# Where the own keys of a second attention get their norm: in the projection stage, or as a factor on the scores

## The chip, the core and the metric

The kernel runs on one core of one Trainium2 chip. The time is the device time of one execution in microseconds. The kernel before took 2516.35 us (median of three runs, 2516.21 to 2521.84 us).

## The reference, cut to what matters

One decoder layer on 8 sequences of 100 tokens with 1024 features: a retention block, a second attention over a context of 722 tokens and the 100 own tokens, and a gated feed-forward block, each with a residual sum and a layer norm. The change is in the second attention. It has 16 query heads and 4 key heads of 128 features:

```python
q = rms_norm((x @ wq).reshape(B, L, 16, 128), q_norm_w)
k = rms_norm((x @ wk).reshape(B, L, 4, 128), k_norm_w)
k_ctx = rms_norm((h_ctx_kv @ wk_ctx).reshape(B, T, 4, 128), k_norm_w)
q = q * cos + rotate_half(q) * sin
k = k * cos + rotate_half(k) * sin
k_full = concatenate([k_ctx, k], axis=1)      # 722 + 100 keys
scores = einsum('blhd,bmhd->bhlm', q, k_full) / sqrt(128) + mask
out = einsum('bhlm,bmhd->blhd', softmax(scores), v_full) @ wo
```

`rms_norm` divides a key by the root of the mean of its squares and multiplies by a weight for each feature. The division is one number per key. The rotation keeps lengths, so this number can be applied to the key before or after the rotation, or to the scores of that key.

## The kernel before

Activations lie with features on the 128 partitions and tokens along the free side: 800 tokens in two halves of 400 columns (4 sequences each). A projection is eight steps over the features, and each step is three matmuls (lines 86 to 88 in `mm3`), because every operand is held as a high and a low part; `split2` (lines 67 and 68) makes the two parts, the high one by a cast on ScalarE and the low one by a subtraction on VectorE. Weights are read by `load_w` into a staging tile `wst` and split into `w`, or, where they were split before, read by `load_ws` straight into `w` (line 82). The stages follow each other: first attention, its output projection, the projection stage of the second attention (lines 618 to 649, 604 to 858 us of the trace), the context stage (lines 655 to 759, 858 to about 1600 us), its output projection, and the feed-forward block.

**The projection stage** loops over four key heads `kv`. For each it projects four query blocks (`i` 0 to 3), one block of own keys (`i == 4`) and one of own values (`i == 5`), each for both halves. For a query or key block: ScalarE squares the result in PSUM (line 640), GpSimd adds the squares over the partitions into `ss` (`all_red`, line 125; `ss` has two buffers), `rope` rotates (lines 133 to 137: two copies on ScalarE, three operations on VectorE, table `tq` or `tk`), `inv_root` makes the inverse root of `ss` (three activations on ScalarE, lines 113, 116 and 118, and two operations on VectorE, lines 119 and 120), and one VectorE operation multiplies (line 645). Then the result is split into `d` and stored: `qd` for queries, `kd` for own keys (line 649). Parts of the context's work for the first two key heads are placed in this stage too (`early`, lines 624 to 628).

**The context stage** loops over 8 sequences `b` and 4 key heads. `context_keys` (lines 587 to 605) projects the 722 context tokens into `kall` without a norm, adds their squares into the tile `kss` (one buffer; `ss` in the code), and stores partition 0 of it as `row` in DRAM: 6 rows of 128 numbers, of which the last 46 are set to one by GpSimd (line 594). Own keys are read from `kd` into the last 100 columns of `kall` (line 672). Lines 687 to 698 read `row` back turned, as a column of 6 numbers on each partition (`rr`), and make the factor `rk` from it. The tile `rk` was set to one at the start; line 698 writes the sixth column only in the first 82 partitions. The scores of 822 keys come in seven chunks of up to 128 keys on the partitions: chunks 0 to 4 are context keys, chunk 5 holds 82 context keys and 46 own keys, chunk 6 holds 54 own keys. They are taken in the order 6, 5, 0 to 4. Each is moved out of PSUM with its factor: chunk 6 and 5 on VectorE with the mask added (line 713; the factor is the constant 1.0 for chunk 6 and the sixth column of `rk` for chunk 5), the others on ScalarE (line 717). Softmax, the product with the values and the store of `o2d` follow.

[...]three under the name `a`, four under `s`, one under `v`. Projections of the projection stage use `a` and `s` in turn.

**What sets the order.** The order of instructions on each engine is not written by hand. A planner takes the program with its dependencies and walks it along a simulated time line with its own cost of each instruction; it gives each engine, and the queue of DMA issues on SyncE (SP), one fixed order. Instructions of one iteration so stand between those of the one before. An engine, and SP, works through its list in order: an instruction that waits holds up all behind it.

Of the kernel before, what the change touches and what calls it, by code (L numbers as in the profile page):

```python
# [8 lines left out]
F32 = mybir.dt.float32  # L9
FR = mybir.dt.float32r  # L10
AF = mybir.ActivationFunctionType
ALU = mybir.AluOpType
# [4 lines left out]
P = 128  # L17
B, T, D = 8, 100, 1024
# [4 lines left out]
SC, SH = 722, 362  # L23
SN = [SH, SC - SH]
NC = 7
ORDER = (6, 5, 0, 1, 2, 3, 4)
C5 = SC - 5 * P
# [4 lines left out]
NKV = 4  # L32
# [7 lines left out]
def decoder_layer(ctx, tc, xT, cT, w1, wo1, w2, wo2, wc, w3, wd, gw, qw, kw, trig, dec, mask, out):  # L40
    nc = tc.nc
# [4 lines left out]
    cp = ctx.enter_context(sbuf("const", 1))  # L46
# [12 lines left out]
    def bt(ap):  # L59
        return ap.rearrange("p (b t) -> p b t", b=NB)  # L60
# [49 lines left out]
    def inv_root(pool, ss, eps, n=N, pin=False):  # L110

        r = pool.tile([P, n], F32, tag="r0", name="r0")
        ln = nc.scalar.activation(r, ss, AF.Ln, bias=eps)
        if pin:
            tc.keep_in_program_order(ln)
        nc.scalar.activation(r, r, AF.Exp, scale=-0.5)
        q = pool.tile([P, n], F32, tag="r1", name="r1")
        nc.scalar.activation(q, r, AF.Square)  # L118
        nc.vector.scalar_tensor_tensor(q, ss, eps, q, ALU.add, ALU.mult)  # L119
        nc.vector.scalar_tensor_tensor(q, q, 3.0, r, ALU.subtract, ALU.mult)  # L120
        return q
# [31 lines left out]
    qd = dr.tile([NKV, 4, P, B, 2, T], FR, name="qd")  # L153
    kd = dr.tile([NKV, P, B, 2, T], FR, name="kd")
    vd = dr.tile([NKV, T, B, 2, P], FR, name="vd")
    o2d = dr.tile([B, P, NKV, 4, 2, T], FR, name="o2d")
    zd = dr.tile([2, P, KT, N], F32, name="zd")
    zd2 = dr.tile([2, P, KT, N], F32, name="zd2")
# [24 lines left out]
    eps_k = const(128e-6, "eps_k")  # L183
    rks = []
    for i in range(2):
        rk = cp.tile([P, 6], F32, name=f"rk{i}")
        nc.vector.memset(rk, 1.0)
        rks.append(rk)
    msk = cp.tile([P, 2, T], F32, name="msk")
    wts = cp.tile([P, 4], F32, name="wts")  # L190
    gws = cp.tile([P, 2], F32, name="gws")
# [4 lines left out]
    def load_constants(p, trg):  # L196
        dcy = p.tile([T, NH1, T], F32, name="dcy", bufs=1)
        nc.sync.dma_start(out=dcy, in_=dec)
        nc.sync.dma_start(out=msk, in_=mask)
        nc.sync.dma_start(out=wts[:, 0:2], in_=gw)  # L200
        nc.sync.dma_start(out=wts[:, 2:3], in_=qw)
        nc.sync.dma_start(out=wts[:, 3:4], in_=kw)

        nc.vector.tensor_scalar(gws, wts[:, 0:2], -8.0, None, ALU.mult)
        nc.vector.tensor_scalar(kws, wts[:, 3:4], -0.5 * math.sqrt(P), None, ALU.mult)
        nc.vector.tensor_scalar(tq, trg[:, 2:4], wts[:, 2:3], None, ALU.mult)
        nc.vector.tensor_scalar(tk, trg[:, 2:4], wts[:, 3:4], None, ALU.mult)
        for t in (tq, tk):
            sw = p.tile([P, T], F32, tag="vt", name="sw", bufs=1)
            nc.vector.tensor_copy(sw, t[:, 1])  # L210
            nc.vector.tensor_copy(t[0:P // 2, 1], sw[P // 2:P])
            nc.vector.tensor_copy(t[P // 2:P, 1], sw[0:P // 2])
        return dcy
# [370 lines left out]
                split(z[k // QT][:, :, k % QT:k % QT + 2, :n], cs)  # L584
            cz.append(z)

    def context_keys(kv):

        kall = ka.tile([P, 2, SC + T], FR, tag="kall", name="kall")
        wk = load_ws(2 * kv)  # L590
        sq = ka.tile([P, SC], F32, tag="ksq", name="ksq", bufs=1)
        ss = ka.tile([P, 6 * P], F32, tag="kss", name="kss", bufs=1)
        row = dr.tile([6, P], F32, tag="row", name="row", bufs=2)
        nc.gpsimd.memset(ss[:, SC:], 1.0)

        def step(hf):
            n, at = SN[hf], slice(hf * SH, hf * SH + SN[hf])
            acc = proj(wk, cz[hf], n)
            nc.scalar.activation(sq[:, at], acc, AF.Square)  # L599
            nc.gpsimd.partition_all_reduce(ss[:, at], sq[:, at], P, RED.add)  # L600
            nc.scalar.activation(kall[:, 0, at], acc, AF.Copy, scale=kws)
            nc.vector.scalar_tensor_tensor(kall[:, 1, at], acc, kws, f32(kall[:, 0, at]), ALU.mult, ALU.subtract)
            if hf:
                nc.sync.dma_start(out=row.rearrange("c p -> (c p)")[None, :], in_=ss[0:1])
        return step, (kall, row)
# [12 lines left out]
    with sbuf("l2", 2) as p:  # L618
        for kv in range(NKV):
            for i0, i1 in ((0, 4), (4, 6)) if kv == 0 else ((0, 2), (2, 4), (4, 6)):  # L620
                if (kv, i0) == (0, 4):
                    load_context(0)
                ws = [load_w(w2[kv, i]) for i in range(i0, i1)]
                if (kv, i0) in ((1, 2), (2, 2)):
                    step, kept = context_keys(kv - 1)
                    early.append(kept)
                if (kv, i0) in ((1, 2), (2, 0), (2, 2), (3, 0)):
                    step(i0 == 0)
                for half in range(2):
                    bs = slice(half * NB, (half + 1) * NB)  # L630
                    for i in range(i0, i1):
                        acc = proj(ws[i - i0], z1[half], tag=acc_tag())
                        if i == 5:
                            tr = tokens_first(p, acc).rearrange("p (b d) -> p b d", b=NB)
                            vs = p.tile([T, NB, 2, P], FR, tag="vs", name="vs", bufs=1)
                            split2(vs[:, :, 0], vs[:, :, 1], tr)
                            nc.sync.dma_start(out=f32(vd[kv, :, bs]), in_=f32(vs))
                            continue
                        sq = p.tile([P, N], F32, tag="sq", name="sq")
                        nc.scalar.activation(sq, acc, AF.Square)  # L640
                        ss = all_red(p, sq, "ss")
                        tb = tq if i < 4 else tk
                        t = rope(p, acc, tb[:, 0], tb[:, 1])
                        r = inv_root(p, ss, eps_k)
                        nc.vector.scalar_tensor_tensor(
                            t, t, -0.5 if i < 4 else -0.5 * math.sqrt(P), r, ALU.mult, ALU.mult)
                        d = p.tile([P, NB, 2, T], FR, tag="d", name="d", bufs=3)
                        split2(d[:, :, 0], d[:, :, 1], bt(t))
                        nc.sync.dma_start(out=f32(qd[kv, i, :, bs] if i < 4 else kd[kv, :, bs]), in_=f32(d))
# [5 lines left out]
    with sbuf("cx", 2) as p, sbuf("c1", 1) as p1:  # L655
# [6 lines left out]
        for b in range(B):  # L662
            if b > 0:
                load_context(b)
            for kv in range(NKV):
                if early:
                    kall, row = early.pop(0)
                else:
                    step, (kall, row) = context_keys(kv)
                    step(0)  # L670
                    step(1)
                nc.sync.dma_start(out=f32(kall[:, :, SC:]), in_=f32(kd[kv, :, b]))
# [11 lines left out]
                    src = tr[0:rows, 0:(c1 - c0) * P].rearrange("p (c d) -> p c d", d=P)  # L684
                    split2(vall[0:rows, c0:c1, 0], vall[0:rows, c0:c1, 1], src)

                rr = p.tile([P, 6], F32, tag="rr", name="rr")
                with nc.allow_non_contiguous_dma("a row turned into a column"):
                    nc.sync.dma_start(out=rr, in_=row.rearrange("c p -> p c"))
                r0 = p.tile([P, 6], F32, tag="rr0", name="rr0")  # L690
                nc.scalar.activation(r0, rr, AF.Ln, bias=eps_k)
                nc.scalar.activation(r0, r0, AF.Exp, scale=-0.5)
                r1 = p.tile([P, 6], F32, tag="rr1", name="rr1")
                nc.vector.tensor_tensor(r1, r0, r0, ALU.mult)
                nc.vector.scalar_tensor_tensor(r1, rr, eps_k, r1, ALU.add, ALU.mult)
                rk = rks[kv % 2]
                nc.vector.scalar_tensor_tensor(rk[:, 0:5], r1[:, 0:5], 3.0, r0[:, 0:5], ALU.subtract, ALU.mult)
                nc.vector.scalar_tensor_tensor(rk[0:C5, 5:6], r1[0:C5, 5:6], 3.0, r0[0:C5, 5:6], ALU.subtract, ALU.mult)

                s = p1.tile([P, NC, N], F32, tag="s", name="s")  # L700
                mx = p.tile([P, N], F32, tag="mx", name="mx")
# [4 lines left out]
                for j, c in enumerate(ORDER):  # L706
                    rows, n, t0 = (R6, N6, T6) if c == 6 else (P, N, 0)
                    sp = bank("s")[0:rows, :n]
                    kh, kl = (kall[:, i, c * P:c * P + rows] for i in range(2))
                    mm3(bt(sp), kh, kl, q[:, :, 0, t0:], q[:, :, 1, t0:], True, True)  # L710
                    sc = s[0:rows, j, :n]
                    if c >= 5:
                        nc.vector.scalar_tensor_tensor(
                            bt(sc), bt(sp), rk[:, 5:6] if c == 5 else 1.0,
                            msk[0:rows, c - 5, None, t0:].to_broadcast([rows, 4, T - t0]), ALU.mult, ALU.add)
                    else:
                        nc.scalar.activation(sc, sp, AF.Copy, scale=rk[:, c:c + 1])  # L717
                        nc.vector.tensor_tensor(mx, s[:, 1] if j == 2 else mx, sc, ALU.max)
                    if j == 2:
                        m6 = part(mx, 6)  # L720
                        nc.vector.tensor_tensor(m6, m6, bt(s[0:R6, 0, :N6]), ALU.max)
# [329 lines left out]
```

## Time and profile before

| what | value |
|---|---|
| median of three runs | 2516.35 us (2516.21 to 2521.84) |
| the profiled execution | 2522.74 us, of which the span is 2521.0 us |
| TensorE busy | 2471.7 us (98%) |
| VectorE busy | 1997.9 us (79%) |
| ScalarE busy | 1352.4 us (54%) |
| GpSimd busy | 478.5 us (19%) |
| mean granted TensorE clock | 0.992 |
| DMA | 438.16 MB, 174 GB/s on average |

The span runs from the first instruction of the program to the last end. All times in the text below count from its start. A busy share is an average over stages: what bounds one stage is read from that stage's own stretch. The idle time printed with an instruction is that of its engine just before it, and the name behind the arrow is what ended the wait.

### The profile page before, as it was taken

To read this page: it belongs to the slowest core of one execution; us is meant where nothing else is said; L and a number is where in the kernel's file an instruction comes from. 1 tells how busy PE (TensorE), PEld (TensorE's weight loads), DVE (VectorE), ACT (ScalarE), POOL (GpSimd) and SP (SyncE) were. 2 spreads that over 40 slices of the span, in tenths; PEclk is the share of its full clock that TensorE was granted. 3 is DMA by queue.
4 is the path that set the end of the run, shared out by engine and by line. 5 is a ranking of instruction groups with operands and counts; after the bars stand their busy time and mean duration, and the time that the engine had idled before them with its cause. 6 is when DMAs were issued, how large, how long until landed. Compare 5 with 4: busy or idle time off the path is not lost.

```text
span 2521.0 us, 37223 instructions
## 1 busy us (share of the span) xinstructions
PE 2471.7 (98%) x14042; PEld 2444.5 (97%) x14042; DVE 1997.9 (79%) x3106; ACT 1352.4 (54%) x2272; POOL 478.5 (19%) x234
## 2 busy tenths in 40 slices
PE   8999999999899999999999999999999999999997
PEld 8999999999899999999999999999999999998996
DVE  7678876568989799999999999867987777666655
ACT  6667676335767456556656556533554444432222
POOL 0111111002655344433433433100000000000000
PEclk9999999999999999999999999999999999999998
DMA  7333445774444654555555554574454444397742
GB/s 240 110 110 127 136 144 187 238 270 147 141 154 134 203 180 137 177 165 161 168 165 154 168 179 150 178 275 147 160 179 176 164 170 158 120 325 290 256 134 78
DMA packets 232898, 438.16 MB, mean 174 GB/s; under 512 B 47594, under 2 KB 176490, under 8 KB 220302
## 3 DMA queue, kind: packets, MB, share of 16 engines
q1 hardware_dynamic: 231566, 431.59, 51.0%
q0 software_dynamic: 1152, 4.19, 1.0%
q8 instruction: 110, 1.80, 0.3%
q14 instruction: 70, 0.57, 0.1%
HBM read 326.38 MB, written 109.35 MB: 173 GB/s over the span
## 4 chain that ended last, share of the span: by engine, by line
PE 89%; DVE 6%; DMA 1%; issue 1%; ACT 1%; SPq 0%; DVEq 0%; ACTq 0%
PE a L88 18%; PE a L86 18%; PE a L87 18%; PE s L88 10%; PE s L87 9%; PE s L86 9%; PE v L87 2%; PE v L88 2%; PE v L86 2%; PE s L486 1%; PE s L683 1%; DVE r L120 1%; DVE r L119 1%; PE s L148 1%; DMA tp<-in_xT 1%
## 5 line engine op out<-in xcount | busy, mean ns | idle before, releaser
L86 PE MATMUL a<-big,w 128*128 128x400 f32 (+2 forms) x1824 | 617.1, 339 | 11.2 <-ACT big L67 6.9
L87 PE MATMUL a<-big,w 128*128 128x400 f32 (+2 forms) x1824 | 616.8, 338 | 0.0
L88 PE MATMUL a<-big,w 128*128 128x400 f32 (+2 forms) x1824 | 615.4, 338 | 0.0
L67 ACT CAST w<-wst 128x1024 fp32r<-128x1024 f32 (+1 forms) x243 | 251.8, 1039 | 428.2 <-PE s L88 152.3
L68 DVE TENSOR_TENSOR w<-wst,w 128x1024 fp32r<-128x1024 f32 (+1 forms) x243 | 295.4, 1218 | 118.6 <-ACT w L67 117.3
L86 PEld LDWEIGHTS a<-big,w 128*128 128x128 f32 x1824 | 344.4, 189 | 13.1 <-ACT big L67 7.3
L87 PEld LDWEIGHTS a<-big,w 128*128 128x128 f32 x1824 | 344.9, 189 | 1.4 <-DVE big L68 0.3
L88 PEld LDWEIGHTS a<-big,w 128*128 128x128 f32 x1824 | 345.0, 189 | 0.9 <-DVE w L68 0.2
L86 PE MATMUL s<-big,w 128*128 128x400 f32 x680 | 236.0, 347 | 0.1
L87 PE MATMUL s<-big,w 128*128 128x400 f32 x680 | 234.7, 345 | 0.0
L88 PE MATMUL s<-big,w 128*128 128x400 f32 x680 | 234.6, 346 | 0.0
L125 POOL PARTITION_ALL_REDUCE ss<-sq x56 | 161.1, 2882 | 336.9 <-DMA zd<-y 167.3
L600 POOL PARTITION_ALL_REDUCE kss<-ksq x64 | 170.6, 2665 | 118.1 <-ACT ksq L599 116.4
L86 PE MATMUL a<-z,w 128*128 128x400 f32 x504 | 174.1, 345 | 8.1 <-ACT r L118 4.3
L88 PE MATMUL a<-z,w 128*128 128x400 f32 x504 | 174.9, 347 | 0.7 <-DVE w L68 0.7
L87 PE MATMUL a<-z,w 128*128 128x400 f32 x504 | 174.8, 347 | 0.0
L87 PE MATMUL s<-z,w 128*128 128x400 f32 x416 | 144.6, 348 | 2.5 <-DVE z L68 2.5
L86 PE MATMUL s<-z,w 128*128 128x400 f32 x416 | 145.3, 350 | 0.0
L88 PE MATMUL s<-z,w 128*128 128x400 f32 x416 | 144.8, 348 | 0.0
L717 ACT ACTIVATE s<-s,rk 128x400 f32<-128x400 f32 x160 | 87.7, 591 | 92.0 <-DVE sm L737 66.1
L86 PEld LDWEIGHTS s<-big,w 128*128 128x128 f32 x680 | 127.6, 188 | 1.4 <-ACT w L67 0.4
L87 PEld LDWEIGHTS s<-big,w 128*128 128x128 f32 x680 | 127.6, 188 | 1.1
(277 smaller groups left out, 5561.4 us busy)
## 6 DMA issues: line engine op xcount, KB each, us to landing
wst<-in_w SPq DMA_DIRECT2D x135, 512.0 KB
w<-wcd SPq DMA_DIRECT2D x64, 1024.0 KB
wst<-in_wo SPq DMA_DIRECT2D x64, 512.0 KB
wst<-in_wd SPq DMA_DIRECT2D x80, 256.0 KB
hd<-h SPq DMA_DIRECT2D x12, 1400.0 KB
big<-o1d SPq DMA_DIRECT2D x16, 800.0 KB
qd<-d SPq DMA_DIRECT2D x32, 400.0 KB
q<-qd SPq DMA_DIRECT2D x32, 400.0 KB
```

Source lines behind the costliest of these rows:

```text
L67: nc.scalar.copy(hi, src)
L68: nc.vector.tensor_tensor(lo, src, f32(hi), ALU.subtract)
L86: nc.tensor.matmul(acc, lh, rh, start=start, stop=False, skip_group_check=chain)
L87: nc.tensor.matmul(acc, lh, rl, start=False, stop=False, skip_group_check=chain)
L88: nc.tensor.matmul(acc, ll, rh, start=False, stop=stop, skip_group_check=chain)
L119: nc.vector.scalar_tensor_tensor(q, ss, eps, q, ALU.add, ALU.mult)
L120: nc.vector.scalar_tensor_tensor(q, q, 3.0, r, ALU.subtract, ALU.mult)
L125: nc.gpsimd.partition_all_reduce(y, x, P, op)
L148: nc.tensor.transpose(tr[0:T, b * P:(b + 1) * P], vt[:, b * T:(b + 1) * T], ident)
L486: nc.tensor.matmul(bt(o)[:, b], vv[:, b * P:(b + 1) * P], pf[:, b], start=True, stop=True)
L600: nc.gpsimd.partition_all_reduce(ss[:, at], sq[:, at], P, RED.add)
L717: nc.scalar.activation(sc, sp, AF.Copy, scale=rk[:, c:c + 1])
```

## The change

The own keys are rotated with a table that holds the factor of the key weight and of the root of 128 (`tk` times `kws` in place of `tk` times the key weight), then split and stored without a norm. Their sums of squares, already made by GpSimd, are stored to a new DRAM tile `ksd`, 400 numbers for each half. In `context_keys`, 100 of these numbers are read into `kss` behind the 722 of the context; GpSimd sets only the remaining 74 to one, on one partition. `row` and everything made from it has seven columns in place of six, and the scores of chunks 5 and 6 take their factor from the sixth and seventh column of `rk`. `rk` is no longer set to one at the start, and one operation writes it in place of two.

```diff
+    ksd = dr.tile([NKV, B, T], F32, name="ksd")
...
-        rk = cp.tile([P, 6], F32, name=f"rk{i}")
-        nc.vector.memset(rk, 1.0)
-        rks.append(rk)
+        rks.append(cp.tile([P, NC], F32, name=f"rk{i}"))
...
-        nc.vector.tensor_scalar(tk, trg[:, 2:4], wts[:, 3:4], None, ALU.mult)
+        nc.vector.tensor_scalar(tk, trg[:, 2:4], kws, None, ALU.mult)
...
-    def context_keys(kv):
+    def context_keys(b, kv):
...
-        ss = ka.tile([P, 6 * P], F32, tag="kss", name="kss", bufs=1)
-        row = dr.tile([6, P], F32, tag="row", name="row", bufs=2)
-        nc.gpsimd.memset(ss[:, SC:], 1.0)
+        ss = ka.tile([P, NC * P], F32, tag="kss", name="kss", bufs=1)
+        row = dr.tile([NC, P], F32, tag="row", name="row", bufs=2)
+        nc.gpsimd.memset(ss[0:1, SC + T:], 1.0)
+        nc.sync.dma_start(out=ss[0:1, SC:SC + T], in_=ksd[kv, b][None, :])
...
-                        r = inv_root(p, ss, eps_k)
-                        nc.vector.scalar_tensor_tensor(
-                            t, t, -0.5 if i < 4 else -0.5 * math.sqrt(P), r, ALU.mult, ALU.mult)
+                        if i < 4:
+                            r = inv_root(p, ss, eps_k)
+                            nc.vector.scalar_tensor_tensor(t, t, -0.5, r, ALU.mult, ALU.mult)
+                        else:
+                            nc.sync.dma_start(out=ksd[kv, bs].rearrange("b t -> (b t)")[None, :], in_=ss[0:1])
...
-                rr = p.tile([P, 6], F32, tag="rr", name="rr")
+                rr = p.tile([P, NC], F32, tag="rr", name="rr")
...
-                nc.vector.scalar_tensor_tensor(rk[:, 0:5], r1[:, 0:5], 3.0, r0[:, 0:5], ALU.subtract, ALU.mult)
-                nc.vector.scalar_tensor_tensor(rk[0:C5, 5:6], r1[0:C5, 5:6], 3.0, r0[0:C5, 5:6], ALU.subtract, ALU.mult)
+                nc.vector.scalar_tensor_tensor(rk, r1, 3.0, r0, ALU.subtract, ALU.mult)
...
-                            bt(sc), bt(sp), rk[:, 5:6] if c == 5 else 1.0,
+                            bt(sc), bt(sp), rk[0:rows, c:c + 1],
```

`NC` is 7. The tiles `rr0` and `rr1`, the name of the second loop's call and the first call of `context_keys` (now with sequence 0) follow in the same way.

More of the change, by code (lines that the diff above doesn't have):

```diff
@@ L624, in decoder_layer @@
                 if (kv, i0) in ((1, 2), (2, 2)):
-                    step, kept = context_keys(kv - 1)
+                    step, kept = context_keys(0, kv - 1)
                     early.append(kept)
@@ L668, in decoder_layer @@
                 else:
-                    step, (kall, row) = context_keys(kv)
+                    step, (kall, row) = context_keys(b, kv)
                     step(0)
@@ L685, in decoder_layer @@
                     split2(vall[0:rows, c0:c1, 0], vall[0:rows, c0:c1, 1], src)
-                rr = p.tile([P, 6], F32, tag="rr", name="rr")
+                rr = p.tile([P, NC], F32, tag="rr", name="rr")
                 with nc.allow_non_contiguous_dma("a row turned into a column"):
                     nc.sync.dma_start(out=rr, in_=row.rearrange("c p -> p c"))
-                r0 = p.tile([P, 6], F32, tag="rr0", name="rr0")
+                r0 = p.tile([P, NC], F32, tag="rr0", name="rr0")
                 nc.scalar.activation(r0, rr, AF.Ln, bias=eps_k)
                 nc.scalar.activation(r0, r0, AF.Exp, scale=-0.5)
-                r1 = p.tile([P, 6], F32, tag="rr1", name="rr1")
+                r1 = p.tile([P, NC], F32, tag="rr1", name="rr1")
                 nc.vector.tensor_tensor(r1, r0, r0, ALU.mult)
```

## The prediction

> **What bounds the kernel now.** I read the page's busy times first, then the busy times by stage, then the idle times of TensorE in order of time, then what stands in the queues there.
>
> ```profile
> span 2521.0 us, 37223 instructions
> PE 2471.7 (98%) x14042; PEld 2444.5 (97%) x14042; DVE 1997.9 (79%) x3106; ACT 1352.4 (54%) x2272; POOL 478.5 (19%) x234
> ```
>
> TensorE is busy 98% of the span, and the change takes no matmul away. So it can gain only idle time of TensorE and the slow matmuls behind such idle time. The table by stage (stretch, its length, then the busy time of TensorE, weight loads, VectorE, ScalarE, GpSimd, and the granted clock) says where there is any:
>
> ```profile
> 604.00:650.00 46.00, 38.49 (x193) 37.18 (x192) 45.34 (x66) 34.28 (x67) 25.89 (x8) 0.93 0.41 140
> 650.00:720.00 70.00, 62.80 (x330) 61.33 (x329) 68.34 (x98) 48.19 (x94) 36.78 (x12) 0.95 0.42 140
> 720.00:835.00 115.00, 114.61 (x641) 114.13 (x639) 105.22 (x148) 82.54 (x158) 63.76 (x25) 1.00 0.45 154
> 835.00:858.00 23.00, 20.62 (x116) 20.01 (x117) 11.95 (x29) 8.57 (x21) 3.67 (x4) 0.93 0.86 276
> 858.00:1590.00 732.00, 732.00 (x4427) 726.62 (x4426) 666.10 (x1153) 443.82 (x852) 289.94 (x151) 1.00 0.52 167
> ```
>
> The context stage (858 to 1590) has no idle TensorE at all: less work on VectorE there is worth nothing, and only a new wait could show. In the projection stage VectorE is the tight engine at first: 113.7 of the 116 us from 604 to 720. From 720 to 835 TensorE is. The waits of TensorE after 650, each with what ended it:
>
> ```profile
> 677.23 0.55 PE L86 MATMUL a<-big,w 128*128 128x362 f32 x1 [2.19 <-DMA w<-wcd]
> 701.51 0.45 PE L86 MATMUL a<-z,w 128*128 128x400 f32 x1 [1.55 <-ACT w L67]
> 714.41 0.64 PE L148 MATMUL s<-ident,vt 128*100 128x128 f32 x4 [2.77 <-ACT vt L145]
> 851.00 0.44 PE L683 MATMUL s<-ident,cvt 128*128 128x128 f32 x2 [1.87 <-ACT cvt L613]
> ```
>
> With 0.69 us at 702.8 and 0.75 us at 835.4 they sum to 9.8 us. Behind the waits at 677, 714 and 851, matmuls start every 0.333 us in place of 0.182 for some 12 matmuls: 1.45, 1.64 and 1.35 us more by the starts in the trace. So 14.3 us are lost after 650. The waits of 2.50 us at 608.5 and 4.32 us at 636.0 come before the first own key reaches VectorE (first operation with `tk`: 655.3 us) and stay.
>
> [...]0.333 us against 0.182, for 3.3 to 4 us; a wait of 1.55 us did not bring it about, one of 1.87 us did. [...]the operations of lines 119, 120 and 645 take 0.62, 0.57 and 0.57 us in the median, 2.1 us at most, and one such long one stands beside most of GpSimd's sums (2.7 us in the median). [...]here the 3 KB store of `row` issued at 1091.84 lets the next read go at 1093.43, so 1.6 us.
>
> **The change part by part.**
>
> *Removed from the projection stage.* Eight blocks of own keys (four heads, two halves) lose three activations (0.63 + 0.54 + 0.54 = 1.7 us) and three VectorE operations. Undisturbed these are 0.62 + 0.57 + 0.57 = 1.75 us; by the means of the 40 in the stage, [...]0.66 + 0.85 + 0.90 = 2.4 us. [...]1.75 is the low end, 2.4 the high end, and I take 2.1. In all 17 us of VectorE and 14 us of ScalarE go. But only what goes before 720 us can shorten the stretch that VectorE bounds: the two blocks of the first head, stored at 671 and 673 us; the second head's are rotated from 711 us on. That is 2 x 2.1 = 4.2 us (3.5 to 4.8). The other six blocks lie where TensorE is busy without a break (720 to 835) or at the tail, where VectorE is busy 12 of 23 us: worth 0.4 us, half of the wait at 835.4. What is late next is the same VectorE queue, now with rotations and weight splits alone.
>
> *The queue of SP at 671 us.* Here an own key's store stands ahead of a weight load that TensorE then waits for:
>
> ```profile
> 670.92 0.32 SPq L649 DMA_DIRECT2D kd<-d  x1
> 671.33 0.38 SPq L82 DMA_DIRECT2D w<-wcd  x1
> ```
>
> The load needs 5.9 us (671.33 to 677.23). This key's rotation ended at 664.6 us (line 137) and its split at 670.9. Without the norm in between, the split can follow the rotation within 1 to 2 us, so some 4 us sooner, and the load with it. The wait of 2.19 us and its slow matmuls (1.45 us) then fall. I do not add these 3.6 us to the 4.2: while VectorE bounds the stretch, TensorE waits elsewhere for what it does not wait for here. They are two sights of one gain.
>
> *Added on SP.* Eight stores of `ksd` of 0.24 us (like `row`'s) to 0.32 us (like `kd`'s) of SP's time, each waiting for GpSimd's sum, and 32 reads into `kss`. A store's wait is short where the planner puts it after the sum; behind it stand the stores of `qd` and reads of weights. A read must wait until the store of the previous `row` has read `kss`. SP waits for that same landing already, for the read of `rr`, 24 times, 40.0 us in total:
>
> ```profile
> SPq L689 <- DMA row<-kss: 40.0, 24, 3.1
> ```
>
> So I cost it at its issue, 0.3 us each, under the prefetch of weights. Were that cover gone, it is up to 1.6 us each. None of it can be a gain. The new read also waits for the landing of `ksd`, written long before. The first store of own keys at 671 and the first `row` at 730 leave room of more than 50 us.
>
> *Buffers.* `ss` has two buffers, and GpSimd waited 38.5 us for line 119 to free one. An own key's buffer is now freed by a DMA: [...]nothing taken, at worst the rival below.
>
> *The column of factors.* `rr` grows from 768 to 896 numbers of 4 bytes. From issue to use the transfer took 5.0 us at 1093.43[...]. The small operations on it grow by a column: nothing. One VectorE operation of 0.15 us goes from each of 32 iterations, under a full TensorE: nothing. The factor of chunk 6 is now a wait that was not there. It comes from the pair of counts:
>
> ```profile
> L697 DVE SCALAR_TENSOR_TENSOR rk<-rr,rr x32: 143/156/967, 850.6 to 1596.4; 128x5 f32<-128x5 f32 x32
> L713 DVE SCALAR_TENSOR_TENSOR s<-s,msk x32: 364/368/376, 857.6 to 1602.9; 54x216 f32<-54x216 f32 x32
> L713 DVE SCALAR_TENSOR_TENSOR s<-s,rk,msk x32: 612/617/634, 863.3 to 1603.2; 128x400 f32<-128x400 f32 x32
> ```
>
> Taken one by one in order, each factor is ready 6.3 us or more ahead of chunk 6 of its iteration (6.8 in the first, 6.3 in the last, 17 us and more in all between, an iteration ahead). So the new wait costs nothing, up to 6 us of lateness. The operation itself costs the same: chunk 5, with a factor per partition, takes 1.54 ns a column, chunk 6 with a constant 1.70.
>
> *Small things.* Two memsets at the start go (0.06 us each); the memset of 0.14 us on GpSimd loses columns; `tk` waits for a tiny product. Nothing.
>
> **Sum.** -4.2 - 0.4 = -4.6 us. The profiled execution (span 2521.0, with 1.74 us around it 2522.74) would take 2518.1 us. It lies 6.4 us above the median of the runs; from the median, 2516.35 - 4.6 = 2511.7 us. The ends: -3.5 with nothing at the tail and 0.6 us more of `rr` ahead of the wait at 851 (2513.5), and -4.8 with the whole 0.75 us (2510.8). A new order from the planner, which sees fewer operations and places all anew, can move single waits of 2 to 4 us with their slow matmuls: about one either way, 2508 to 2516.
>
> **Rivals.**
>
> *All waits fall.* The waits after 650 us are all one backlog on VectorE and ScalarE, and the relief clears it. For: three of the six end on ScalarE, whose queue stood behind VectorE (36.3 us for line 645 alone). Against: the wait at 851 follows a `rr` read. Gain 14.3 us: 2502.1 us.
>
> *Slower: SP holds the `ss` buffers.* SP works in order and waits 105.1 us in 32 times for splits ahead of `qd` and `kd` stores, 3.3 us each. If a `ksd` store stands behind one, its buffer stays taken 3.3 us longer, GpSimd's next sum starts late, the Ln that needs it waits at the head of ScalarE's queue, and behind it stand the copies that free TensorE's banks. Each case that reaches TensorE costs 3.3 + 1.5 us. One eats the gain of 4.6; from three on it is slower by over 0.3%; four of the eight give 19.2 - 4.6 = 14.6 us more: 2531 us. Against: the sum is ready before the rotated key is split, so the planner has reason to place the store early.
>
> *It does nothing.* TensorE's waits move to weight loads and casts that the relief does not touch: 2516 us.
>
> **How the numbers follow.** Forecast 0.38, all waits fall 0.33, nothing 0.14, SP holds buffers 0.15. Three thousandths, 7.5 us, are about what a measurement of this kernel can tell from no change. Faster by more: nearly all of the second case and the low tail of the first, 0.38. Within: 0.47. Slower by more: 0.15. The range 2500 to 2526 us takes in the forecast, most of the second case and the mild end of the slower one; about 0.07 lie below and 0.12 above. Where own ranges are asked for, the forecast's is 2508 to 2516.
>
> **What would show it.** Right: line 645 and lines 113 to 120 run 32 times in place of 40; no wait for `w<-wcd` near 675; fewer or shorter waits of TensorE up to 720; none in the context stage; `rk` still an iteration ahead of chunk 6. Wrong: SP waiting for GpSimd's sums with stores behind it, GpSimd waiting for `ksd` landings, TensorE idle after 858, or TensorE's waits before 720 as long as now under other names.

## The result and the profile after

| | before | after |
|---|---|---|
| median (six runs each) | 2518.76 us (2516.21 to 2521.84) | 2542.60 us (2537.11 to 2545.04) |
| profiled execution, its span | 2522.74 us, 2521.0 us | 2544.87 us, 2543.1 us |

The ratio is 1.0089, with a 95% interval of 1.0079 to 1.0100. The change makes the kernel 23.8 us slower. The forecast was 2511.7 us, and the range ended at 2526.

First the busy times of the kernel after, from the head of its page:

```profile
span 2543.1 us, 37234 instructions
PE 2480.0 (98%) x14042; PEld 2449.7 (96%) x14042; DVE 1999.6 (79%) x3048; ACT 1338.8 (53%) x2248; POOL 480.0 (19%) x234
```

TensorE runs the same 14042 matmuls. VectorE has 58 instructions fewer and ScalarE 24: eight norms of three operations on each are gone, and on VectorE the 32 second writes of `rk` and two memsets with them. The total shows no reason for a longer time. The table by stage of the kernel after does (the columns are those of before: stretch, length, then TensorE, weight loads, VectorE, ScalarE, GpSimd, clock):

```profile
604.00:650.00 46.00, 38.78 (x192) 37.73 (x191) 45.33 (x66) 35.46 (x69) 25.41 (x8) 0.89 0.39 134
650.00:720.00 70.00, 65.26 (x352) 64.83 (x351) 65.56 (x91) 45.44 (x87) 37.96 (x13) 0.95 0.47 154
720.00:835.00 115.00, 114.59 (x640) 114.11 (x640) 102.23 (x143) 77.19 (x148) 61.34 (x24) 1.00 0.44 150
835.00:858.00 23.00, 21.06 (x129) 20.41 (x128) 7.50 (x20) 6.72 (x17) 3.98 (x5) 1.00 0.94 303
858.00:1590.00 732.00, 716.31 (x4272) 706.75 (x4272) 655.49 (x1083) 425.21 (x825) 286.59 (x148) 0.99 0.48 154
```

Read the counts of matmuls. Up to 858 us TensorE has started 1313 since 604 us, against 1280 before: the projection stage is 33 matmuls ahead. In the context stage it starts 4272 against 4427: 155 fewer in the same 732 us. At 732 / 4427 = 0.165 us each, that is 25.6 us of work not yet done. The gain came, and the next stage lost nearly five times as much. TensorE, never idle there before, now is for 732 - 716.3 = 15.7 us. Its waits from 858 to 1590 us, by what ended them (total, times, longest), begin so; the same view of before has no line:

```profile
PE a L86 <- DVE kall L603: 9.6, 6, 1.8
PE a L86 <- ACT big L67: 1.9, 2, 1.0
```

The split of `kall` on VectorE (line 603) frees a PSUM bank of the name `a` for the next projection. In order of time, with the projection stage's longest wait ahead of them, each with its start, its duration and the idle time before it:

```profile
678.20 0.67 PE L86 MATMUL a<-big,w 128*128 128x362 f32 x1 [4.74 <-DMA w<-wcd]
...
1212.67 0.43 PE L86 MATMUL a<-big,w 128*128 128x360 f32 x1 [1.79 <-DVE kall L603]
1313.83 0.43 PE L86 MATMUL a<-big,w 128*128 128x360 f32 x1 [1.80 <-DVE kall L603]
1412.20 0.67 PE L86 MATMUL a<-big,w 128*128 128x360 f32 x1 [1.80 <-DVE kall L603]
1514.43 0.67 PE L86 MATMUL a<-big,w 128*128 128x360 f32 x1 [1.80 <-DVE kall L603]
```

One wait of nearly the same length comes about every 100 us, once in four iterations, that is once for each sequence (1.61 us at 1114.9 and 0.78 us at 1041.5 begin the row). Behind three of the four shown, matmuls of 360 columns start every 0.30 us in place of 0.167. Against the same matmuls behind the fourth, at 1313.8 us, that is 1.5, 2.5 and 2.6 us more, 6.6 us in all. Idle time and slow matmuls make 22.3 of the 25.6 us; the rest is not assigned, since a count of matmuls of several lengths is no finer.

**What stands in the way at 1313.8 us.** TensorE in the kernel after, up to that wait:

```profile
1309.51 0.49 PE L686 MATMUL s<-ident,cvt 128*128 128x128 f32 x3
1310.55 0.79 PE L686 MATMUL s<-ident,cvt 128*128 128x128 f32 x3 [0.55 <-ACT s L719]
1311.52 0.31 PE L86 MATMUL s<-q,kall 128*54 128x216 f32 x1 [0.18 <-ACT s L719]
...
1313.83 0.43 PE L86 MATMUL a<-big,w 128*128 128x360 f32 x1 [1.80 <-DVE kall L603]
```

VectorE in the kernel after at the same place:

```profile
1304.40 1.78 DVE L739 TENSOR_TENSOR sm<-sm,s 128x400 f32<-128x400 f32 x3
1306.22 0.98 DVE L715 SCALAR_TENSOR_TENSOR s<-s,rk,msk 54x216 f32<-54x216 f32 x2
...
1308.96 1.89 DVE L720 TENSOR_TENSOR mx<-mx,s 128x400 f32<-128x400 f32 x1
...
1313.20 0.58 DVE L603 SCALAR_TENSOR_TENSOR kall<-a,kws,kall 128x362 fp32r<-128x362 f32 x1
```

And ScalarE:

```profile
1306.28 1.08 ACT L719 ACTIVATE s<-s,rk 128x400 f32<-128x400 f32 x2 [4.74 <-DVE sm L739]
```

The row is to be read backwards. TensorE waits for the split at 1313.20. VectorE came to it late: eight operations of the softmax stand ahead of it from 1307.3 on, and VectorE has no idle time among them. Three additions of the iteration before (line 739) stand together just ahead of chunk 6's move, and so ahead of all eight. ScalarE waited 4.74 us for those additions before it could refill the tiles that they read, and the transposes wait for ScalarE in turn. In the kernel before, the same step of an iteration, on TensorE, looks like this:

```profile
1110.47 0.49 PE L683 MATMUL s<-ident,cvt 128*128 128x128 f32 x3
1110.72 0.41 PE L87 MATMUL a<-big,w 128*128 128x360 f32 x1
...
1113.10 0.38 PE L683 MATMUL s<-ident,cvt 128*128 128x128 f32 x2
1113.23 0.41 PE L86 MATMUL a<-big,w 128*128 128x360 f32 x1
```

Here key projections of the next iteration (`a<-big,w`) stand between the transposes and cover whatever these wait for. After the change the transposes stand together, the projections are done either sooner or later, and nothing covers the wait. Of all the instructions shown here the diff touches chunk 6's move alone; the others do what they did before, in another order.

### The profile page after: what moved, and what is told of

The parts are those of the page before. It is cut to its first block, busy times and chain, and to the rows that moved or that the text cites. A ratio compares the mean times of both kernels' runs of the same rounds, so it can differ in the third digit from the quotient of the medians.

```text
span 2543.1 us, 37234 instructions
## 1 busy us (share of the span) xinstructions
PE 2480.0 (98%) x14042; PEld 2449.7 (96%) x14042; DVE 1999.6 (79%) x3048; ACT 1338.8 (53%) x2248; POOL 480.0 (19%) x234
## 4 chain that ended last, share of the span: by engine, by line
PE 77%; DVE 11%; DMA 5%; ACT 3%; issue 3%; POOL 1%; SPq 0%; DVEq 0%; ACTq 0%; POOLq 0%
PE a L86 15%; PE a L88 15%; PE a L87 15%; PE s L88 9%; PE s L87 9%; PE s L86 9%; DVE sm L739 2%; DMA cs<-in_cT 1%; DMA rr<-row 1%; PE s L485 1%; DVE pl L68 1%; PE v L88 1%; PE v L86 1%; PE v L87 1%; DVE mx L720 1%
## 5 line engine op out<-in xcount | busy, mean ns | idle before, releaser
L86 PEld LDWEIGHTS a<-big,w 128*128 128x128 f32 x1824 | 346.7, 190 | 30.9 <-DVE kall L603 11.0
L601 POOL PARTITION_ALL_REDUCE kss<-ksq x64 | 175.0, 2736 | 315.7 <-ACT ksq L600 315.7
L125 POOL PARTITION_ALL_REDUCE ss<-sq x56 | 159.1, 2848 | 329.7 <-DMA zd<-y 167.0
```

The source lines that it names most:

```text
L86: nc.tensor.matmul(acc, lh, rh, start=start, stop=False, skip_group_check=chain)
L125: nc.gpsimd.partition_all_reduce(y, x, P, op)
```

## The experiments

The theories. **P**: the diff moves the planner to another order of the context stage, and that order costs the time. **W**: chunk 6 waits for its factor. **K**: the new stores and reads of `ksd` hold SP, or `kss`. **N**: taking the norm out of the projection stage moves something into the context stage. **F** (formed after the first runs): not the order but the form of chunk 6's operation on VectorE, with a factor for each partition, holds VectorE. All times are medians; that of the runs of before on the same chip is beside them. The ratio is the recorded one. For e5 to e8, with seven runs of before on their chip, it lies up to 0.11% above the quotient of the two columns.

| run | us | before | ratio (95%) |
|---|---|---|---|
| `e1_chunk6_constant` | 2515.18 | 2518.79 | 0.9983 (0.9976 to 0.9990) |
| `e2_chunk6_ready_column` | 2541.59 | 2518.79 | 1.0097 (1.0081 to 1.0112) |
| `e3_scores_alone` | 2540.23 | 2518.79 | 1.0085 (1.0068 to 1.0102) |
| `e4_norm_left_out` | 2514.74 | 2518.79 | 0.9983 (0.9975 to 0.9990) |
| `e5_no_new_dma` | 2542.79 | 2521.28 | 1.0089 (1.0070 to 1.0108) |
| `e6_form_kept_other_order` | 2670.28 | 2521.28 | 1.0595 (1.0579 to 1.0612) |
| `e7_chunk6_on_scalar` | 2537.01 | 2521.28 | 1.0073 (1.0057 to 1.0090) |
| `e8_before_ready_column` | 2540.60 | 2521.28 | 1.0087 (1.0071 to 1.0104) |
| `e9_copies_swapped` | 2513.14 | 2519.04 | 0.9976 (0.9966 to 0.9986) |
| `e10_scalar_chunk6_square` | 2511.17 | 2519.04 | 0.9969 (0.9959 to 0.9980) |
| `e11_before_copies_swapped` | 2519.78 | 2519.89 | 0.9996 (0.9987 to 1.0006) |
| `e12_own_keys_from_query_store` | 2514.82 | 2519.89 | 0.9980 (0.9973 to 0.9987) |

**e1: after, with the constant back at chunk 6.** Everything else of the change stays, the DMAs and the seven columns too.

```diff
-                            bt(sc), bt(sp), rk[0:rows, c:c + 1],
+                            bt(sc), bt(sp), 1.0 if c == 6 else rk[0:rows, c:c + 1],
```

> The changed kernel, but chunk 6 leaves PSUM with the constant 1.0 again (the 54 own keys of chunk 6 are left without their norm). All else of the change stays: the stores of ksd, the reads into kss, seven columns, no norm in the projection stage. Theory P (the form of chunk 6's operation makes the planner choose another order of the context stage, and that order is worse): the time falls by 24 to 28 us against the changed kernel, to about 2515 to 2519, TensorE has no idle time in the context stage. Rival K (the new DMAs on SP and the column of seven): stays at 2541 to 2545. Rival W (chunk 6 waits for rk): falls as under P.

Measured 2515.18 us: one operand, with the order that it brings, is worth 2542.6 - 2515.2 = 27.4 us, and the rest of the change is a small gain. K falls with this run.

**e2: after, chunk 6 with a column of ones.** The column is a fifth one in the tile of weights, set at the start. The form of the operation is that of after, but it depends on nothing of its iteration.

```diff
+    nc.vector.memset(wts[:, 4:5], 1.0)
-                            bt(sc), bt(sp), rk[0:rows, c:c + 1],
+                            bt(sc), bt(sp), rk[0:rows, c:c + 1] if c == 5 else wts[0:rows, 4:5],
```

> The changed kernel, but chunk 6 takes its factor from a column of ones that is set at the start, so it has the form of the changed kernel and waits for no rk (its own keys are left without their norm). Its compiled order on TensorE and ScalarE is that of the changed kernel, instruction for instruction. Theory P: 2541 to 2545, as the changed kernel. Rival W (the wait for rk): falls to 2515 to 2519. Rival K: 2541 to 2545.

Measured 2541.59 us, as slow as after, with no factor to wait for. W falls. TensorE's and ScalarE's compiled orders are the same as in after, instruction by instruction: it is the operand's kind that changes the order, not its dependency.

**e3: the factors on the scores alone.** The own keys keep their norm in the projection stage, nothing is stored to `ksd`, and `row` is set to one behind the context's keys.

```diff
-        nc.gpsimd.memset(ss[0:1, SC + T:], 1.0)
-        nc.sync.dma_start(out=ss[0:1, SC:SC + T], in_=ksd[kv, b][None, :])
+        nc.gpsimd.memset(ss[0:1, SC:], 1.0)
-                        if i < 4:
-                            r = inv_root(p, ss, eps_k)
...
-                            nc.sync.dma_start(out=ksd[kv, bs].rearrange("b t -> (b t)")[None, :], in_=ss[0:1])
+                        r = inv_root(p, ss, eps_k)
+                        nc.vector.scalar_tensor_tensor(t, t, -0.5, r, ALU.mult, ALU.mult)
```

> The scores' part alone: own keys keep their norm in the projection stage, no ksd, nothing read into kss (the own keys' numbers in it are ones), but seven columns and chunks 5 and 6 both take rk. Theory P: the context stage is as slow as in the changed kernel or near it (its order is near but not the same), and the projection stage keeps its waits: 2535 to 2550. Rival K (DMAs of ksd): 2516 to 2521, as before. Rival N (the norm's leaving shifts the stages): 2516 to 2521.

Measured 2540.23 us. The loss is there with the norm in its old place: N falls, and K a second time.

**e4: before, with the own keys' norm simply dropped.** This measures the relief of the projection stage by itself.

```diff
-                        r = inv_root(p, ss, eps_k)
...
+                        if i < 4:
+                            r = inv_root(p, ss, eps_k)
+                            nc.vector.scalar_tensor_tensor(t, t, -0.5, r, ALU.mult, ALU.mult)
```

> The kernel before with the own keys' norm left out of the projection stage and nothing put in its place (own keys go without a norm); six columns, the constant for chunk 6. It is the relief of the projection stage alone. Theory P and the prediction's own step: 2510 to 2516, the context stage without idle TensorE. Rival N (the lighter projection stage makes the planner choose the bad order): 2535 to 2545.

Measured 2514.74 against 2518.79 us: 4.05 us, where 4.6 were forecast for the relief.

**e5: after, without the new stores and reads.**

```diff
-        nc.gpsimd.memset(ss[0:1, SC + T:], 1.0)
-        nc.sync.dma_start(out=ss[0:1, SC:SC + T], in_=ksd[kv, b][None, :])
+        nc.gpsimd.memset(ss[0:1, SC:], 1.0)
-                            nc.sync.dma_start(out=ksd[kv, bs].rearrange("b t -> (b t)")[None, :], in_=ss[0:1])
+                            pass
```

> The changed kernel without the stores of ksd and without the reads into kss (the own keys' numbers in kss are ones, so own keys go without their norm). Chunks 5 and 6 take their factor from rk. Its compiled order on TensorE is that of the changed kernel. Theory P (the order of the context stage costs the time): 2540 to 2545. Rival K (the 40 new DMAs on SP, or what waits behind them): 2512 to 2519.

Measured 1.0089 times before, the ratio of after itself. The DMAs cost nothing that shows. The first runs bound it closer: e1 has the DMAs and the seventh column, e4 has neither, and they lie 0.4 us apart on one chip (2515.18 and 2514.74).

**e6: after, with the square of `rr` on GpSimd.** It was meant to give the planner another order at the same form.

```diff
-                nc.vector.tensor_tensor(r1, r0, r0, ALU.mult)
+                nc.gpsimd.tensor_tensor(r1, r0, r0, ALU.mult)
```

> The changed kernel with one small operation moved: the square of rr0 (128x7) is made by GpSimd in place of VectorE. All of the change stays, chunk 6's factor per partition and the new DMAs too. The planner then gives TensorE nearly the order of the run with the constant (e1). Theory P, order alone: 2513 to 2519, no idle TensorE after 860 us but the first few. Rival F (chunk 6's operation with a factor per partition is itself what costs, 434 ns against 368, on the path of the scores): 2538 to 2545.

Measured 2670.28 us, a miss by over 150 us, and so no test of the order: the edit has a cost of its own. GpSimd's waits in this run (total, times, longest):

```profile
POOL rr L697 <- issue: 202.9, 27, 9.1
...
POOL mb L125 <- issue: 91.3, 15, 8.3
```

The square itself takes 0.2 us. GpSimd stands 7.5 us in the mean ahead of it and 6.1 us ahead of the next sum over the partitions, with nothing to wait for. At the same line the trace has 62 instructions named `MODIFY_POOL_CONFIG`, on GpSimd's sequencer:

```profile
L697 POOLq MODIFY_POOL_CONFIG  x62: 1/1/90, 837.5 to 1736.3; - x62
```

What this instruction does no run shows. Besides the 62 at the squares, 64 stand at the lines of the sums (54 at L125, 10 at L601); the whole kernel before has 4. With 32 squares, that is about two for each change between the two kinds of operation in e6, which goes with these waits.

**e7: after, chunk 6 moved by ScalarE.** ScalarE multiplies by the factor as it does for chunks 0 to 4, and VectorE adds the mask. No operation of VectorE on chunk 6 has a factor any more.

```diff
-                    if c >= 5:
+                    if c == 6:
+                        nc.scalar.activation(sc, sp, AF.Copy, scale=rk[0:rows, c:c + 1])
+                        nc.vector.tensor_tensor(bt(sc), bt(sc), msk[0:rows, 1, None, t0:].to_broadcast([rows, 4, T - t0]), ALU.add)
+                    elif c == 5:
```

> The changed kernel with chunk 6 moved out of PSUM by ScalarE with its factor, and the mask added by VectorE afterwards (tensor_tensor). There is no VectorE operation with a factor per partition for chunk 6 any more. TensorE's compiled order is near the changed kernel's, not e1's. Theory P, order alone: slow, 2530 to 2550. Rival F: 2513 to 2522.

Measured 2537.01 us. TensorE's waits in the context stage begin with the same kind as in after:

```profile
PE a L86 <- DVE kall L603: 8.4, 5, 1.9
```

Four of the five come at 1204.8, 1305.9, 1404.9 and 1503.7 us, 1.74 to 1.95 us each: once in a sequence again. That is what P expects, but it does not rule F out alone. VectorE's addition of the mask takes 1.28 us in the mean here, where the single operation of after takes 0.434, so VectorE is not relieved. e9 and e10 decide.

**e8: before, with the column of ones at chunk 6.** It computes the same numbers as before and has nothing of the change.

```diff
-                            bt(sc), bt(sp), rk[:, 5:6] if c == 5 else 1.0,
+                            bt(sc), bt(sp), rk[:, 5:6] if c == 5 else wts[0:rows, 4:5],
```

> The kernel before with chunk 6's constant 1.0 replaced by a column of ones set at the start: the same numbers come out, nothing else is changed. The planner gives a third order, between the two. Theory P: the time moves by an amount that only this order decides, I expect slower by 5 to 25 us (2524 to 2544). Rival F (the operation's own 66 ns): 32 x 0.066 = 2 us at most, 2519 to 2521, if TensorE bounds the stage as before.

Measured 2540.60 us: 19.3 us more than before on its chip (2521.28), 0.87% by the ratio. The operation on chunk 6 takes 0.434 us with a factor for each partition and 0.368 with a constant: 32 x 0.066 = 2.1 us, if all of it showed. The remaining 17 us at least are the order.

**e9: after, with two copies swapped.** For each head, the values of the two halves are copied out of PSUM, one by ScalarE and one by VectorE. This edit swaps which takes which; the work is the same, and so is the change.

```diff
-            copy = nc.scalar.copy if hf == 0 else nc.vector.tensor_copy
+            copy = nc.vector.tensor_copy if hf == 0 else nc.scalar.copy
```

> The changed kernel with the two copies of the context values' projection exchanged: VectorE copies the first half and ScalarE the second. The work of each engine is the same to within two columns of 362, chunk 6 keeps its factor per partition (434 ns), and all new DMAs stay. The planner gives TensorE an order like e1's: 96 separate groups of transposes in the 32 iterations, where e1 has 94, the kernel before 97 and the changed kernel 83. Theory P, order alone: 2510 to 2520, no waits of TensorE for the split of context keys (kall) in the context stage. Rival F (chunk 6's dearer operation on the path of the scores): 2538 to 2545.

Measured 2513.14 us: 29.5 us less than after, and 5.9 less than before on the same chip. The stage's line of e9 shows TensorE full again and 150 matmuls more than after in it:

```profile
858.00:1590.00 732.00, 732.00 (x4422) 726.86 (x4421) 669.89 (x1129) 449.92 (x856) 282.69 (x150) 1.00 0.52 166
```

No wait of TensorE is left between 860 and 1640 us. The form of chunk 6 and its factor are those of after. F falls: the order decides.

**e10: e7, with the square of `rr` on ScalarE.** The same operations for chunk 6 as in e7, in another order.

```diff
-                nc.vector.tensor_tensor(r1, r0, r0, ALU.mult)
+                nc.scalar.activation(r1, r0, AF.Square)
```

> The kernel of e7 (chunk 6 on ScalarE with its factor, mask added on VectorE) with one more small edit: the square of rr0 (128x7) on ScalarE in place of VectorE. The planner now gives TensorE an order like that of the kernel before (96 groups of transposes; e7 has 87). Theory P, order alone: 2510 to 2522, some 20 us less than e7 with the same operations for chunk 6. Rival G (what moves chunk 6 costs, by its added work on ScalarE and VectorE): 2534 to 2541 as e7.

Measured 2511.17 us, 25.8 less than e7. It is the fastest version measured, 0.31% under before, and holds the whole change. VectorE's addition on chunk 6 in e10 (shortest, median and longest in ns):

```profile
L716 DVE TENSOR_TENSOR s<-s,msk x32: 362/1480/1716, 852.1 to 1592.5; 54x216 f32<-54x216 f32 x32
```

The longest form of chunk 6's operation on VectorE stands in the fastest kernel. G falls, and F once more.

**e11: before, with the same swap as e9.**

> The kernel before with the two copies of the context values' projection exchanged as in e9, nothing of the change. It tells whether e9's gain comes from the exchange or from the change. Its order on TensorE has 98 groups of transposes, like the kernel before. Theory P with the relief of the projection stage as the change's own worth: 2517 to 2521, as before (e9 is then 4 to 7 us faster by the change). Rival X (the exchange itself gains): 2510 to 2515.

Measured 0.9996 times before: the swap by itself is worth nothing. So e9's 5.9 us come with the change. How much of them is the relief (3.6 us in e1, 4.05 in e4) and how much one more order, the runs do not separate.

**e12: e4, with the own keys read from another store.** In e4, `kall`'s read of `kd` stands on SP ahead of the weight load that TensorE waits for. This one takes the same number of bytes from `qd`, written long before, so that it need not wait for the store of `kd`; the own keys are left out of the scores.

```diff
-                nc.sync.dma_start(out=f32(kall[:, :, SC:]), in_=f32(kd[kv, :, b]))
+                nc.sync.dma_start(out=f32(kall[:, :, SC:]), in_=f32(qd[kv, 0, :, b]))
```

> The kernel of e4 (own keys' norm left out), and the own keys in kall are read from the store of a query block in place of kd (other numbers, written long before). SP's read into kall then has no landing of kd to wait for. Its compiled order on TensorE is e4's. If the weight load at 669 us stands behind that read's wait on SP: SP's wait of 3.85 us goes, the load is issued 2 to 4 us sooner, TensorE's wait for w<-wcd (3.96 us at 676.6 in e4) falls to 0 to 2 us, and the time to 2508 to 2513. If something else holds the load (a free buffer of w, the second kd store's data): that wait and the time stay, 2513 to 2516.

Measured 2514.82 us against e4's 2514.74. TensorE's wait for the load in e4, then two of its waits in e12:

```profile
676.59 0.67 PE L86 MATMUL a<-big,w 128*128 128x362 f32 x1 [3.96 <-DMA w<-wcd]
...
675.49 0.43 PE L86 MATMUL a<-big,w 128*128 128x362 f32 x1 [1.44 <-DMA w<-wcd]
...
710.11 1.09 PE L148 MATMUL s<-ident,vt 128*100 128x128 f32 x4 [2.78 <-ACT vt L145]
```

Neither forecast came out whole. SP's wait for the landing went, but the second store of `kd` then held SP, and the load was issued 0.4 us later than in e4 (669.74 against 669.35). The wait for it fell all the same, from 3.96 to 1.44 us, and the one for `vt`, gone in e4, came back with 2.78. What is won at one wait is lost at the next. That VectorE sets the pace of the stretch fits this, busy for 65.9 of the 70 us from 650 to 720 in e12, but no run tests it alone.

**One feature parts the runs.** In the compiled order of TensorE one can count how often transposes of `cvt` begin anew between other matmuls in the 32 iterations. Before has 97 such groups, e1 94, e4 94, e12 94, e9 96, e10 96, e11 98, and these are the seven with 2511 to 2520 us. After, e2 and e5 have 83, e3 87, e7 87, e8 85, and these are the six with 2537 to 2543 us. e6 (94) takes long for its own reason. The count tells the two orders apart. The traces show the same more sharply. In these six there are places where all six transposes of an iteration follow each other with no other matmul between: five each in after, e2 and e5, four each in e3, e7 and e8. The seven others have none, nor has e6. Behind each of these 27 places, within 4 us, stands a wait of TensorE for the split of `kall`, 1.56 to 2.14 us long. That the bunched transposes alone cost the time is still not shown: the rest of the order changes with them.

## Why the prediction was wrong, point by point

**Right.** *The relief of the projection stage*, -4.6 us: e4 gave -4.05, e1 -3.6, e9 -5.9. In e4 TensorE is 30 matmuls ahead of before at 720 us and 39 at 858, so most of the gain falls in the stretch that the forecast named. In the kernel after the waits at 701 and 714 us are gone and TensorE is 33 matmuls ahead at 858. The 2.1 us for a block was an estimate between 1.75 and 2.4. From 604 to 858 us, 35 of VectorE's 296 operations on 128x400 take 1.22 to 2.18 us in the kernel before, each within one of GpSimd's 44 sums, and the others 0.56 to 0.73. In the kernel after it is 35 of 272, again each within a sum, of 1.12 to 2.18 us and with 65.5 us in all against 65.7. So the long ones did not become fewer, and other operations are among them. *The new DMAs cost nothing*: e5 equals after, and e1 lies 0.4 us from e4. SP waited 12.3 us in 5 times for GpSimd's sums, with nothing late behind it that shows. GpSimd's wait for a free `ss` stayed at 38.6 us against 38.5, so the slower rival, SP holding these buffers, is not what happened; that its sign came true is luck. *The new wait for the factor costs nothing*: it is ready 7.5 us ahead in the first iteration and 21 us or more later, and e2, which has no such wait, is as slow. The 0.6 us for the longer `rr` was an estimate that the traces do not bear out: where ScalarE waited for it, `rr` took 2.13 to 7.57 us from issue to use in the kernel before (13 times, 4.48 in the median) and 2.12 to 7.17 in the kernel after (26 times, 2.40).

**Wrong in a small thing: the load at 671.** The own keys' store was to go some 4 us sooner and the load of `w` with it. SP's queue in the kernel after:

```profile
663.88 2.71 SPq L652 DMA_DIRECT2D kd<-d  x1
669.99 0.37 SPq L675 DMA_DIRECT2D kall<-kd  x1
670.45 0.42 SPq L652 DMA_DIRECT2D kd<-d  x1
670.97 0.38 SPq L82 DMA_DIRECT2D w<-wcd  x1
```

The first store did go 7 us sooner. The load stayed at 671, since a read and the second store stand ahead of it, and the read waits 3.4 us for the landing of the first; the second store, whose split ended at 668.95 us, came behind it, at 670.45. TensorE came 1.6 us sooner (673.5 against 675.0 us) and the load's data 1.0 us later: its wait grew from 2.19 to 4.74 us. As the prediction had not added this wait to its sum ("two sights of one gain"), the sum held; e12 fits the reason. Two readings of the trace of before were off and changed nothing: behind 677 and 851 us the matmuls have 362 columns and start every 0.30 us in place of 0.167, and four of the six waits, not three, end on ScalarE.

**The step that failed** is the last of the sum: "A new order from the planner ... can move single waits of 2 to 4 us with their slow matmuls: about one either way, 2508 to 2516." With it fails "only a new wait could show", which was asked of the new factor alone. The context stage is one plan repeated: a place where TensorE waits for a bank once in a sequence is paid for each sequence again, in the kernel after from 1114 us on. Idle time and slow matmuls there came to 22.3 us (15.7 + 6.6), not to one wait of 4. The term was mis-sized by the number of repeats, and no rival had it. e8 measures it without the rest of the change, +19.3 us on its chip; e9 and e10 take it away with the whole change kept, -29.5 and (against e7) -25.8 us.

**What tripped it** was costed as "The operation itself costs the same", from a time per column of two operations of different width. On the chip that was nearly true: 0.368 to 0.434 us, 2.1 us in all. But e1 and e2 show that the operand's kind alone, a constant or a number for each partition, decides between the two orders. A sum of the operation's time on the chip cannot see that.

The error of 30.9 us so splits: 2.4 us for the median of before, 2516.35 in three runs and 2518.76 in six; 1.0 us for the change without its last operand (e1, 2515.18, against 2518.76 - 4.6 = 2514.2); 27.4 us for the last operand, of which the operation's own time is 2.1 us at most and the order the rest.

**Open.** Why the planner's own costs lead from this operand to that order was not traced. Which difference in the order costs the time, the additions ahead of chunk 6, the bunched transposes or the late projections, was not taken apart: each experiment changes the whole order. And what a third order might give is not bounded by two that were seen; the seven runs of the first kind lie within 9 us.

## What to carry to other kernels

In a kernel whose order a planner writes, cost an edit twice: what its instructions take, and what a new order can do to each stage that repeats, one wait times its repeats, on both sides of zero. A stage that is full without a gap has only loss to show there. Before a difference is put down to what a diff computes, compare an edit that computes the same numbers. Here a column of ones moved the kernel before by +0.87% and two swapped copies the kernel after by -1.2%, more than the change itself is worth; the same swap moved the kernel before by nothing.

## What the runs showed of the hardware

GpSimd's change between a product of two tiles and a sum over the partitions (e6): 32 products of 0.2 us made the kernel 149 us longer than before on its chip and 128 us longer than after. A move of 54 x 216 numbers out of PSUM took 0.434 us with a factor for each partition and 0.368 us with a constant. Of four waits of TensorE of 1.79 and 1.80 us, three were followed by matmuls at the slower pace (granted clock 0.50 from 1412 to 1416 us) and one, at 1313.8 us, was not (1.00 from 1313.8 to 1317). Nor was one of 1.61 us, at 1114.9 (1.00 from 1114.9 to 1118). Behind the three the slower pace lasted until 1216.4, 1417.8 and 1520.3 us: 3.7, 5.6 and 5.9 us from the end of the wait. What decides whether it comes, and for how long, these traces do not tell.
